# Moving the x_r product of a graph attention layer from the node phase into the rounds of edges, and loading x first

## The chip, the cores and the metric

The kernel runs on one core of a Trainium2 chip. A core has five engines with queues of their own: PE (matrix products and transposes into PSUM), DVE (vector operations), ACT (activations), POOL (general work, and here also the issuing of gathers) and SP (issuing of the other DMAs). Each engine executes its instructions in the order in which they were written down, and waits on semaphores for the others. The metric is the device time of one execution in microseconds (us). Before the change it is 4172.99 us, the median of 3 runs (4167.11 to 4175.78).

## What is computed

A graph attention layer (GATv2) with a feed-forward block, over 12500 nodes of 128 features and 400000 edges that are sorted by their destination. Cut to what matters:

```
h  = max(layernorm(x), 0)
n  = layernorm(h) * ln1_g + ln1_b
x_l = n @ W_l ;  x_r = n @ W_r          # 8 heads of 16 channels
for each edge (src -> dst), and for a loop at each node:
    m     = leaky_relu(x_l[src] + x_r[dst] + edge_attr @ W_e, 0.2)
    alpha = sum over channels of m * att, per head
a   = softmax of alpha over the edges that end in a node
h2  = h + sum of a * x_l[src] + bias
out = x + h2 + gelu(layernorm(h2) @ W1 + b1) @ W2 + b2
```

Nodes are padded to 98 tiles of 128. All of it is computed in float32; x_r is stored as three bfloat16 parts whose sum is the float32 value.

## The kernel before

The kernel has two phases. The **node phase** (lines 509 to 551) computes x_l and x_r of all nodes and writes them to DRAM: x_l to `xl_dram` (as float32, with ones behind it), x_r to `xs_dram` (as three bfloat16 parts). The **rounds of edges** (`window_edges`, lines 634 to 1132) then go over the edges, 512 in each of 782 rounds.

The order of work on every engine is written out by hand. Both phases are a loop over rounds, and a table of stages says how many rounds after its first one a group of nodes, or a batch of edges, passes through each step. Within a round the steps run in the order of the table.

In the node phase a group is four tiles (25 groups, the last with two tiles). The table `node_stages` has: `x_stats` (DVE, mean and variance of x), `x_mean`, `relu` (ACT, layer norm and relu in one operation per tile, with the row sum), `h_mean`, `h_turn` (PE, four transposes), `h_turned` (the copy out of PSUM, on DVE for odd groups and ACT for even ones), `h_square` (ACT), `h_var` (DVE), `product` (PE, against W_r and W_l side by side, 256 columns), `x_lr` (DVE, one operation per tile over 256 columns, line 477, and the store of x_l by SP, line 485) and `split` (POOL, five operations that make the three bfloat16 parts of x_r, lines 492 to 496, and their store by SP, line 497). Reciprocals and square roots (lines 545 and 547) run ahead of the stages.

Four further pieces of work are put into rounds of the node phase: `weights` (round 3), `from_first` (round 6: DVE converts the destinations, POOL takes two differences of 112x3584, line 340, and SP stores them), `fits` (round 8, DVE: does the fast path hold?) and `edge_constants` (round 10, some 20 small operations of POOL and DVE; the second of DVE, line 291, copies `we_sb`).

The loads are issued by SP in this order: x tiles 0 to 3, x tiles 4 to 15 (`load_x`), the destinations in seven DMAs (`load_dst`, of which line 240 is the large one, with 111 rows of 14 KB, lines 255 and 258 are made of single elements, and line 264 is the last), the other 82 tiles of x in six loads, then the constants (`load_consts`, with `we_sb` in line 222) and the sources of the edges. W_l, W_r, ln1_g and ln1_b are loaded by ACT's queue.

In a round of edges c, POOL gathers 4 x 128 rows of x_l by the edges' sources (`gather`, line 700, four rounds ahead of their use, into a ring of 12 buffers). SP loads, three rounds ahead, the rows of x_r that the batch can end in (`windows`; line 721 loads `xrw` from `xs_dram` at a row number held in a register). PE adds x_l, x_r and the edge term into PSUM (`combine`), ACT and DVE apply the leaky relu (`slope`, `bend`), PE, DVE and ACT compute the weights (`score`, `lowest`, `weigh`), PE transposes them (`turn`, into the ring of two banks `pt_ps`), ACT copies them out (`keep_turned`, line 795), PE sums (`collect`, round 6), DVE picks each head's own part (`own_heads`), and SP stores the result (`put`, line 826).

A second table, `steps`, finishes each group of nodes after its last edge: loop edge, softmax, feed-forward and output, in 20 rounds (`f_load` to `f_store`). Between rounds 0 and 200 the sum of all edge attributes is taken on the side.

Of the kernel before, what the change touches and what calls it, by code (L numbers as in the profile page):

```python
# [13 lines left out]
F32 = mybir.dt.float32  # L14
# [8 lines left out]
H = 8  # L23
# [96 lines left out]
def tile_gnn(  # L120
# [53 lines left out]
    flag = keep.tile([1, 1], I32, name="flag")  # L174

# [23 lines left out]
    lr_ps = pre.enter_context(tc.tile_pool(name="lr_ps", bufs=2, space=PSUM))  # L199
# [9 lines left out]
    quads = [(t, min(GN, NT - t)) for t in range(0, NT, GN)]  # L209
# [60 lines left out]
    wlr = build.tile([P, 2, C, H], F32, name="wlr")  # L270
    bw_r = build.tile([P, 2, C, H], F32, name="bw_r")

    def weights():
        mean = build.tile([P, P], F32, name="mean")
        nc.vector.memset(mean, 1.0 / P)
        b_b = build.tile([P, P], F32, name="b_b")
        nc.scalar.copy(b_b, b1n_c.to_broadcast([P, P]))
        for i, w in enumerate((wr_sb, wl_sb)):
            nc.vector.tensor_scalar(wlr[:, i], w.rearrange("p (h c) -> p c h", c=C), g1_c, None, op0=OP.mult)
        wlr_f = wlr.rearrange("p s c h -> p (s c h)")  # L280
        ps = once_ps.tile([P, 2 * P], F32, name="w_ps")
        nc.tensor.matmul(ps, mean, wlr_f, start=True, stop=True)
        nc.vector.tensor_sub(wlr_f, wlr_f, ps)
        ps = once_ps.tile([P, 2 * P], F32, name="w_ps")
        for i, w in enumerate((wr_sb, wl_sb)):
            nc.tensor.matmul(ps[:, i * P : (i + 1) * P], b_b, w, start=True, stop=True)
        nc.vector.tensor_copy(bw_r, ps.rearrange("p (s h c) -> p s c h", s=2, h=H))
# [107 lines left out]
    qs = [{"t0": t, "n": n, "h": h_sb[:, t : t + n, :]} for t, n in quads]  # L395

    roots = {}

    def col(d, name):
        d[name] = node.tile([P, GN], F32, name=f"n_{name}", bufs=5)[:, 0 : d["n"]]  # L400
        return d[name]

    def root_of(d, r, k):
        if r not in roots:
            roots[r] = (node.tile([P, 2, GN], F32, name="n_r", bufs=6), [0, 0])
        t, ns = roots[r]
        ns[k] = d["n"]
        d[f"r{k}"] = t[:, k, 0 : d["n"]]
        return d[f"r{k}"]

    def slots(r):
        if r not in roots:
            return []
        t, ns = roots[r]
        return [t] if ns == [GN, GN] else [t[:, k, 0:n] for k, n in enumerate(ns) if n]
# [14 lines left out]
    def relu(d, r):  # L430
        col(d, "sum")
        for t in range(d["n"]):
            nc.scalar.activation(
                d["h"][:, t, :], d["h"][:, t, :], AF.Relu,
                bias=d["m1"][:, t : t + 1], scale=d["r0"][:, t : t + 1], accum_out=d["sum"][:, t : t + 1],
            )

    def h_mean(d, r):
        nc.vector.tensor_scalar(d["sum"], d["sum"], -1.0 / P, None, op0=OP.mult)
# [14 lines left out]
    def h_square(d, r):  # L454
        col(d, "ssq")
        for t in range(d["n"]):
            sq = node.tile([P, P], F32, name="sq")
            nc.scalar.activation(
                sq, d["h"][:, t, :], AF.Square, bias=d["sum"][:, t : t + 1], accum_out=d["ssq"][:, t : t + 1]
            )  # L460
# [4 lines left out]
    def product(d, r):  # L465
        d["lr"] = lr_ps.tile([P, GN, 2 * P], F32, name="lr")
        for t in range(d["n"]):
            nc.tensor.matmul(
                d["lr"][:, t, :], d["hT"][:, t, :], wlr.rearrange("p s c h -> p (s c h)"), start=True, stop=True
            )  # L470

    def x_lr(d, r):
        n = d["n"]
        d["xlr"] = node.tile([P, GN, P + XW], F32, name="xlr")
        nc.gpsimd.memset(d["xlr"][:, :, 2 * P :], 1.0)
        for t in range(n):
            nc.vector.scalar_tensor_tensor(
                d["xlr"][:, t, 0 : 2 * P],
                d["lr"][:, t, :],
                d["r1"][:, t : t + 1],  # L480
                bw_r.rearrange("p s c h -> p (s c h)"),
                op0=OP.mult,
                op1=OP.add,
            )
        nc.sync.dma_start(xl_t[:, d["t0"] : d["t0"] + n, :], d["xlr"][:, 0:n, P:])

    def split(d, r):
        n = d["n"]
        xr = d["xlr"][:, 0:n, 0:P]
        parts = node.tile([P, GN, NS, P], BF16, name="parts")[:, 0:n]  # L490
        left = node.tile([P, GN, P], F32, name="left")[:, 0:n]
        nc.gpsimd.tensor_copy(parts[:, :, 0, :], xr)
        nc.gpsimd.tensor_sub(left, xr, parts[:, :, 0, :])
        nc.gpsimd.tensor_copy(parts[:, :, 1, :], left)
        nc.gpsimd.tensor_sub(left, left, parts[:, :, 1, :])
        nc.gpsimd.tensor_copy(parts[:, :, 2, :], left)
        nc.sync.dma_start(xs_t[:, d["t0"] : d["t0"] + n, :, :], parts)
# [4 lines left out]
    def clear(g):  # L502
# [12 lines left out]
        (8, x_lr),  # L515
# [5 lines left out]
        (9, split),  # L521
    )
    LAST = 9
    with tc.manual_schedule():
        make_identity(nc, ident)
        load_weights()
        load_x(0, min(GN, NT))
        load_x(GN, min(3 * GN, NT - GN))
        load_dst()
        for t in range(4 * GN, NT, 14):  # L530
            load_x(t, min(14, NT - t))
        load_consts()
        nc.gpsimd.memset(empty, 0.0)
        nc.gpsimd.memset(empty[:, :, C + 1 : SH], CAP)
        for r in range(max(len(qs), 2) + LAST + 1):
            if r == 3:
                weights()
            if r == 6:
                from_first()
            if r == 8:  # L540
                fits()
            if r == 10:
                edge_constants()
            for t in slots(r - 2):
                nc.vector.reciprocal(t, t)
            for t in slots(r - 1):
                nc.scalar.activation(t, t, AF.Sqrt)
            for late, f in node_stages:
                if 0 <= r - late < len(qs):
                    f(qs[r - late], r)  # L550
        clear(0)
# [3 lines left out]
    with tc.If(fast == 1) as cmp:  # L555
        window_edges(
            tc, n_edges, ea_t, NT, NE, NUE, ident, ident_b, wer, we_z, negrep, diag, nid, farw, bias_r, b2_r, w1_sb, w2_sb,
            cols, xl_dram, xl_t, xs_dram, xs_t, dc_dram, du_dram, state, clear, x_t, out_t, h_sb, src_sb, first_sb,
        )
    with cmp.Else():  # L560
        any_edges(
            tc, n_edges, dst, dst_tiles, ea_t, NT, NG, NCH, CPP, CP, ident, w_e, att, att_c, bias_r,
            xl_dram, xl_t, xs_t, h_sb, src_sb,
        )
        feed_forward(tc, NT, NG, ident, b2_r, w1_sb, w2_sb, cols, x_t, out_t, h_sb)
# [68 lines left out]
def window_edges(  # L634
    tc, n_edges, ea_t, NT, NE, NUE, ident, ident_b, wer, we_z, negrep, diag, nid, farw, bias_r, b2_r, w1_sb, w2_sb,
    cols, xl_dram, xl_t, xs_dram, xs_t, dc_dram, du_dram, state, clear, x_t, out_t, h_sb, src_sb, first_sb,
# [29 lines left out]
    with ExitStack() as es:  # L666
        once = es.enter_context(tc.tile_pool(name="e_once", bufs=1))
        load = es.enter_context(tc.tile_pool(name="e_load", bufs=3))
# [80 lines left out]
        def slope(c):  # L749
            d, e = pairs[c], sum(edges_of(c))  # L750
            d["zs"] = work.tile([P, EPR], F32, name="zs")
            nc.scalar.activation(d["zs"][:, :e], d["z"][:, :e], AF.Copy, scale=SLOPE)  # L752
# [292 lines left out]
        def f_store(d):  # L1045
# [10 lines left out]
            (LATE + 1, own_heads),  # L1056
            (0, combine),
# [7 lines left out]
            (5, keep_turned),  # L1065
# [42 lines left out]
        def in_round(r, table):  # L1108
            for k, f in table:
                for d in groups:  # L1110
                    if d["round"] + k == r:
                        f(d)

        CLEAR = 8
        with tc.manual_schedule():
            for r in range(-AHEAD, max(last_round, groups[-1]["round"] + 20)):
                in_round(r, early)
                for late, f in stages:
                    c = r - late
                    if 0 <= c < n_pr:  # L1120
                        f(c)
                for late, f in sum_stages:
                    i, off = divmod(r - late, SUM_STEP)
                    if off == 0 and 0 <= i < NL:
                        f(i)
                if r > 0 and r % CLEAR == 0 and r // CLEAR < NT // GT:
                    clear(r // CLEAR)
                in_round(r, steps)
                for late, f in late_stages:
                    c = r - late  # L1130
                    if 0 <= c < n_pr:
                        f(c)


def any_edges(
    tc, n_edges, dst, dst_tiles, ea_t, NT, NG, NCH, CPP, CP, ident, w_e, att, att_c, bias_r,
    xl_dram, xl_t, xs_t, h_sb, src_sb,
# [31 lines left out]
    with tc.tile_pool(name="build", bufs=1) as build:  # L1169
# [9 lines left out]
        nc.vector.scalar_tensor_tensor(pick, kh, float(LO), high, op0=OP.is_equal, op1=OP.add)  # L1179

# [302 lines left out]
```

## Time and profile before

| | value |
|---|---|
| median of 3 runs | 4172.99 us (4167.11 to 4175.78) |
| the profiled execution | 4170.51 us, of which its span 4168.6 us |
| mean granted PE clock | 0.946 |
| first 200 us: PE, DVE, ACT, POOL busy | 76.8, 135.6, 97.7, 125.9 us |
| 2000 to 2400 us: PE, DVE, ACT, POOL busy | 362.8, 236.0, 180.9, 302.6 us |
| first gather, last gather | start at 190.6 us and 4097.0 us |
| `split` on POOL, 25 of each of five operations | 28.4 + 28.4 + 15.2 + 15.2 + 15.0 us |

The span is the time from the first to the last instruction in the trace; the run's time has a little around it. A row of the profile that names a line gives the engine, the operation, what it writes and reads, how often it ran, its busy time, the mean of one in ns, and the idle time of the engine just before it with what ended that idle time ("releaser"). "issue" is waiting for which the profile shows no cause. A `q` behind an engine's name is its queue: the time in which it issues a DMA. In tables of windows, the columns are the stretch, its length, busy time of the engine with the number of its instructions, the granted PE clock, the share of the 16 DMA engines that is busy, and GB/s.

In the trace of before the row of line 721 stands 782 times, that of line 497 25 times, all of them before 190 us.

### The profile page before, as it was taken

The page shows a single profiled execution, that of the slowest core. Times are in us where ns is not written, and L with a number is a line of the kernel's source. Part 1 is how long each engine was busy: PE and PEld are TensorE (multiplying, and loading weights), DVE is VectorE, ACT ScalarE, POOL GpSimd, SP SyncE. Part 2 cuts the span into 40 slices and gives each one's busy share as a digit, 9 for nine tenths or more (in the row PEclk, how much of TensorE's full clock was granted, in tenths as well). Part 3 has the DMA queues.
Part 4 walks back from the last instruction along what each step waited for, and adds up shares of the span by engine and source line. Part 5 has one row for each costly group of instructions (what it writes and reads, how often), then busy time and mean ns, then how long its engine had stood idle before and what let it go on. Part 6 is the DMA issues. An engine that isn't in the chain of part 4 may idle for free. (4 is left out here: it accounts for less than half of the span.)

```text
span 4168.6 us, 65325 instructions
## 1 busy us (share of the span) xinstructions
PE 3562.9 (85%) x18674; PEld 2472.1 (59%) x18675; DVE 2433.0 (58%) x5279; ACT 1802.9 (43%) x3939; POOL 3073.7 (74%) x3303
## 2 busy tenths in 40 slices
PE   2488888888888898989899989889889999988985
PEld 2355555655566666666666666566666666665654
DVE  6655656656665555655555555565556564655554
ACT  4533333333334444444444444444444444434433
POOL 3977777777777777777777777777777777777772
PEclk8799999999999999999999999999999999999998
DMA  5577777666656555555655566555566565555562
GB/s 150 172 169 182 182 180 179 156 153 159 150 118 116 115 116 119 115 112 115 125 117 117 117 119 120 117 117 105 117 122 118 117 120 113 107 117 104 114 123 51
DMA packets 631298, 535.20 MB, mean 128 GB/s; under 512 B 381763, under 2 KB 520882, under 8 KB 630690
## 3 DMA queue, kind: packets, MB, share of 16 engines
q1 hardware_dynamic: 530354, 313.00, 30.8%
q0 software_dynamic: 100000, 217.80, 29.6%
q8 instruction: 153, 2.51, 0.3%
q14 instruction: 215, 1.76, 0.2%
q10 hardware_dynamic: 576, 0.13, 0.0%
HBM read 477.18 MB, written 53.34 MB: 127 GB/s over the span
## 5 line engine op out<-in xcount | busy, mean ns | idle before, releaser
L700 POOL DMA_INDIRECT xs<-xl_dram,src_sb x3125 | 2955.1, 946 | 952.5 <-issue 808.9
L782 ACT ACTIVATE p<-ab,rec 128x256 f32<-128x256 f32 x1563 | 655.2, 470 | 1678.4 <-DVE rec L771 1654.1
L813 DVE TENSOR_TENSOR own<-acc,diag 128x272 f32<-128x272 f32 x782 | 344.7, 441 | 1360.3 <-PE acc L804 1353.6
L742 PE MATMUL z<-ident,xs 128*128 128x128 f32 x3125 | 585.7, 286 | 474.2 <-DMA xs<-xl_dram,src_sb 467.6
L742 PEld LDWEIGHTS z<-ident,xs 128*128 128x128 f32 x3125 | 405.0, 142 | 945.0 <-DMA xs<-xl_dram,src_sb 563.5
L804 PE MATMUL acc<-xs,pt 128*128 128x136 f32 x6250 | 884.6, 286 | 0.2 <-DVE f_yo L1051 0.2
L746 PE MATMUL z<-ea,we_z 128*128 128x512 f32 x1564 | 859.1, 633 | 0.0
L804 PEld LDWEIGHTS acc<-xs,pt 128*128 128x128 f32 x6250 | 812.5, 197 | 0.4 <-PE pt_ps L790 0.4
L764 PE MATMUL ab<-m,negrep 128*128 128x512 f32 x1564 | 801.1, 594 | 0.0
L752 ACT ACTIVATE zs<-z 128x512 f32<-128x512 f32 x782 | 474.7, 607 | 494.7 <-PE z L746 453.8
L790 PEld LDWEIGHTS pt_ps<-ident,p 128*128 128x128 f32 x3125 | 417.9, 149 | 453.6 <-issue 424.2
L771 DVE TENSOR_REDUCE rec<-ab 128x2 f32<-128x512 f32 x781 | 540.6, 692 | 135.9 <-PE ab L764 128.5
L757 DVE TENSOR_TENSOR m<-z,zs 128x512 f32<-128x512 f32 x782 | 532.2, 681 | 54.2 <-ACT zs L752 54.1
L790 PE MATMUL pt_ps<-ident,p 128*128 128x128 f32 x3125 | 498.2, 285 | 1.7 <-ACT pt L795 1.7
L795 ACT COPY pt<-pt_ps 128x512 f32<-128x512 f32 x782 | 457.6, 585 | 0.0
L819 DVE TENSOR_REDUCE rec<-own 128x34 f32<-128x272 f32 x782 | 341.0, 436 | 26.6
L746 PEld LDWEIGHTS z<-ea,we_z 128*128 128x128 f32 x1564 | 314.6, 201 | 35.7
L764 PEld LDWEIGHTS ab<-m,negrep 128*128 128x128 f32 x1564 | 301.8, 193 | 37.4 <-issue 0.7
L745 PE MATMUL z<-ne,xrw 128*128 128x512 bf16 x782 | 311.3, 398 | 0.0
L728 DVE TENSOR_SCALAR ne<-dlw,nid 112x512 bf16<-112x512 bf16 x782 | 288.5, 369 | 25.6 <-DMA dlw<-du_dram 25.6
L763 PE MATMUL ab<-ne,farw 128*128 128x512 bf16 x782 | 300.9, 385 | 0.0
L839 DVE TENSOR_REDUCE part<-ea_s 128x1 f32<-128x1024 f32 x98 | 118.5, 1209 | 0.0
(165 smaller groups left out, 1619.0 us busy)
## 6 DMA issues: line engine op xcount, KB each, us to landing
dlw<-dc_dram SPq DMA_DIRECT2D x196, 384.0 KB
ea<-in_ea_t SPq DMA_DIRECT2D x196, 256.0 KB
ea_s<-in_ea_t SPq DMA_DIRECT2D x98, 512.0 KB
xs<-xl_dram,src_sb POOLq DMA_INDIRECT x3125
state<-rec SPq DMA_DIRECT2D x1563, 9.0 KB
xrw<-xs_dram SPq DMA_DIRECT2D x782, 24.0 KB
state<-empty SPq DMA_DIRECT2D x28, 504.0 KB
st<-state SPq DMA_DIRECT2D x48, 288.0 KB
```

What stands on the lines that cost most here:

```text
L700: nc.gpsimd.indirect_dma_start(out=xs[:, j, :], out_offset=None, in_=xl_dram, in_offset=bass.IndirectOffsetOnAxis(ap=src_sb[:, c * KP + j ...
L742: nc.tensor.matmul(z[:, j * P : (j + 1) * P], d["xs"][:, j, 0:P], ident, start=(j == 0), stop=False, is_transpose=True)
L746: nc.tensor.matmul(z[:, :e], we_z[:, c % QP, :], d["ea"][:, :e], start=False, stop=True)
L752: nc.scalar.activation(d["zs"][:, :e], d["z"][:, :e], AF.Copy, scale=SLOPE)
L757: nc.vector.tensor_tensor(d["m"][:, :e], d["z"][:, :e], d["zs"][:, :e], op=OP.max)
L764: nc.tensor.matmul(ab[:, :e], negrep.rearrange("p n h -> p (n h)"), d["m"][:, :e], start=False, stop=True)
L771: nc.vector.tensor_reduce(d["rec"][:, :, CX], d["ab"].rearrange("p (u e) -> p u e", e=U), AX.X, OP.min)
L782: nc.scalar.activation(d["p"][:, us], d["ab"][:, us], AF.Exp, bias=d["rec"][:, i, CX:SH], scale=-1.0)
L790: nc.tensor.transpose(d["pt_ps"][:, js], d["p"][:, js], ident)
L795: nc.scalar.copy(d["pt"][:, :e], d["pt_ps"][:, :e])
L804: nc.tensor.matmul(d["acc"][:, i, :], d["pt"][:, j * P : (j + 1) * P], d["xs"][:, j, :], start=(j == js[0]), stop=(j == js[-1]),)
L813: nc.vector.tensor_tensor(own[:, :nu], d["acc"][:, :nu].rearrange("p u (c h) -> p u c h", h=H), diag[:, None].to_broadcast([P, nu, CX, H]) ...
```

## The change

The node phase keeps the x_l half of the product, 128 columns. Its stage `split` is gone; `x_lr` becomes `x_l`. It now keeps two things per group that lived in rotating buffers before: the reciprocal roots (`roots_sb`) and the negative mean of h (`mean_sb`).

A new function `xr_steps` computes x_r of a group from them in eight steps: `norm` (one small DVE product, four ACT operations), `turn` (PE, four transposes), `turned` (ACT, the copy with the affine part of the norm), `times` (PE, four products with W_r), `first` (ACT copy and DVE subtraction), `second` (ACT copy), `third` (DVE subtraction) and `store` (SP). Group 0 goes through them in rounds 8 to 15 of the node phase. The others go through them in the rounds of edges, one step a round, in the ring `pt_ps`: group k starts in round 32k - 18, so that its store is issued two rounds ahead of the first window that can need it.

The load of dst is put behind all loads of x. `edge_constants` moves from round 10 to round 7, `from_first` from 6 to 10, `fits` from 8 to 12. In the rounds of edges `keep_turned` is put ahead of `combine`. The pool `load` shrinks from three buffers to two, `zs` from three to two, and `lr_ps` grows from two to three banks of half the size in use.

```diff
-    lr_ps = pre.enter_context(tc.tile_pool(name="lr_ps", bufs=2, space=PSUM))
+    lr_ps = pre.enter_context(tc.tile_pool(name="lr_ps", bufs=3, space=PSUM))
...
     def product(d, r):
-        d["lr"] = lr_ps.tile([P, GN, 2 * P], F32, name="lr")
+        d["lr"] = lr_ps.tile([P, GN, P], F32, name="lr")
...
-                d["xlr"][:, t, 0 : 2 * P],
+                d["xl"][:, t, 0:P],
...
-    def split(d, r):
-        n = d["n"]
-        xr = d["xlr"][:, 0:n, 0:P]
-        parts = node.tile([P, GN, NS, P], BF16, name="parts")[:, 0:n]
-        left = node.tile([P, GN, P], F32, name="left")[:, 0:n]
-        nc.gpsimd.tensor_copy(parts[:, :, 0, :], xr)
-        nc.gpsimd.tensor_sub(left, xr, parts[:, :, 0, :])
-        nc.gpsimd.tensor_copy(parts[:, :, 1, :], left)
-        nc.gpsimd.tensor_sub(left, left, parts[:, :, 1, :])
-        nc.gpsimd.tensor_copy(parts[:, :, 2, :], left)
-        nc.sync.dma_start(xs_t[:, d["t0"] : d["t0"] + n, :, :], parts)
+    def xr_steps(pool, bank):
+        def norm(d):
+            off = pool.tile([P, GN], F32, name="xr_off")[:, 0 : d["n"]]
+            nc.vector.tensor_mul(off, d["mean"], d["r1"])
+            hn = tile_of(d, "hn", 0)
+            for t in range(d["n"]):
+                nc.scalar.activation(
+                    hn[:, t, :], d["h"][:, t, :], AF.Identity, bias=off[:, t : t + 1], scale=d["r1"][:, t : t + 1]
+                )
+        def turn(d):
+            d["b"] = bank()
+            for t in range(d["n"]):
+                nc.tensor.transpose(d["b"][:, t * P : (t + 1) * P], d["hn"][:, t, :], ident)
+        def turned(d):
+            nc.scalar.activation(
+                tile_of(d, "hT", 1).rearrange("p t f -> p (t f)"),
+                d["b"][:, 0 : d["n"] * P], AF.Identity, bias=b1n_c, scale=g1_c,
+            )
+        def times(d):
+            d["b"] = bank()
+            for t in range(d["n"]):
+                nc.tensor.matmul(
+                    d["b"][:, t * P : (t + 1) * P], d["hT"][:, t, :], wr_c.rearrange("p c h -> p (c h)"),
+                    start=True, stop=True,
+                )
+        def first(d):
+            n = d["n"]
+            xr = d["b"][:, 0 : n * P].rearrange("p (t f) -> p t f", f=P)
+            d["parts"] = pool.tile([P, GN, NS, P], BF16, name="xr_parts")[:, 0:n]
+            nc.scalar.copy(d["parts"][:, :, 0, :], xr)
+            nc.vector.tensor_sub(tile_of(d, "left", 0), xr, d["parts"][:, :, 0, :])
+        def second(d):
+            nc.scalar.copy(d["parts"][:, :, 1, :], d["left"][:, 0 : d["n"]])
+        def third(d):
+            nc.vector.tensor_sub(d["parts"][:, :, 2, :], d["left"][:, 0 : d["n"]], d["parts"][:, :, 1, :])
+        def store(d):
+            nc.sync.dma_start(xs_t[:, d["ts"], :, :], d["parts"])
+        return norm, turn, turned, times, first, second, third, store
...
-        load_dst()
         for t in range(4 * GN, NT, 14):
             load_x(t, min(14, NT - t))
+        load_dst()
         load_consts()
...
-            if r == 6:
+            if r == 7:
+                edge_constants()
+            if r == 10:
                 from_first()
-            if r == 8:
+            if r == 12:
                 fits()
-            if r == 10:
-                edge_constants()
...
+            if 0 <= r - LAST < len(first_xr):
+                first_xr[r - LAST](qs[0])
...
-        load = es.enter_context(tc.tile_pool(name="e_load", bufs=3))
+        load = es.enter_context(tc.tile_pool(name="e_load", bufs=2))
...
-            d["zs"] = work.tile([P, EPR], F32, name="zs")
+            d["zs"] = work.tile([P, EPR], F32, name="zs", bufs=2)
...
             (LATE + 1, own_heads),
+            (5, keep_turned),
             (0, combine),
...
-            (5, keep_turned),
             (-1, place),
...
+        xr_steps = xr_steps(fin, lambda: ps2.tile([P, EPR], F32, name="pt_ps"))
+        per_node = edges_per_node(NT, n_edges)
+        for d in qs[1:]:
+            first = (d["t0"] * P - CW) * per_node // U - SPARE
+            d["round"] = first // UP - WAHEAD - len(xr_steps) - 1
+            assert d["round"] >= -AHEAD
...
                 in_round(r, steps)
+                in_round(r, enumerate(xr_steps), qs[1:])
```

## The prediction

> **What bounds the kernel now.** I read the page's busy times first, then the gathers by stretch, then who waited for whom, then the timeline before the first gather. PE is the busiest engine on the page, and yet the waits show that it is POOL's gathers that pace everything.
>
> ```profile
> PE 3562.9 (85%) x18674; PEld 2472.1 (59%) x18675; DVE 2433.0 (58%) x5279; ACT 1802.9 (43%) x3939; POOL 3073.7 (74%) x3303
> L700 POOL DMA_INDIRECT xs<-xl_dram,src_sb x3125 | 2955.1, 946 | 952.5 <-issue 808.9
> ```
>
> In the windows of line 700 (busy time, instructions, granted clock, DMA share, GB/s) the gathers keep one pace, with or without sums of edge attributes (up to 1200 us) and finishing steps beside them:
>
> ```profile
> 600.00:1000.00 400.00, 302.43 (x321) 0.96 0.71 163
> 1400.00:1800.00 400.00, 302.45 (x321) 0.95 0.60 120
> 3000.00:3400.00 400.00, 302.57 (x320) 0.96 0.60 118
> ```
>
> In the waits, no pause before a gather is longer than 0.3 us, and PE stops for gathered rows:
>
> ```profile
> POOL xs L700 <- issue: 808.9, 2654, 0.3
> PE z L742 <- DMA xs<-xl_dram,src_sb: 467.6, 343, 27.9
> ```
>
> The first gather starts at 190.6 us and the last at 4097.0: 3906.4 us for 3124 steps, 1.2505 us each. So span = start of the first gather + 3906.4 + tail (4168.6 - 4097.0 = 71.6). Only the start can give much, and its timeline (start, duration) shows POOL splitting x_r right up to it:
>
> ```profile
> 177.51 0.61 POOL L492 CAST parts<-xlr 128x512 bf16<-128x512 f32 x1
> 181.93 0.61 POOL L492 CAST parts<-xlr 128x512 bf16<-128x512 f32 x1
> 188.71 0.40 POOL L496 CAST parts<-left 128x256 bf16<-128x256 f32 x1
> 189.45 0.93 POOL L683 MEMSET xrw<- 128x128 bf16 x6 [0.34 <-issue]
> 190.56 1.12 POOL L700 DMA_INDIRECT xs<-xl_dram,src_sb  x1 [0.17 <-issue]
> ```
>
> One group of four tiles costs POOL 4.42 us (177.51 to 181.93); ACT had finished at 161, DVE's last x_lr at 176. The early timeline shows two more stops, the load of dst and a pair of POOL subtractions:
>
> ```profile
> 7.64 22.74 SPq L258 DMA_DIRECT2D lu<-in_dst  x1
> 31.90 12.58 SPq L232 DMA_DIRECT2D h_sb<-in_x  x6
> 36.98 0.29 DVE L421 BATCH_NORM_STATS2 s<-h_sb 128x6 f32<-128x128 f32 x1 [18.94 <-DMA h_sb<-in_x]
> 43.32 12.28 POOL L340 TENSOR_TENSOR dlb<-df 112x3584 bf16<-112x3584 f32 x2 [41.36 <-DVE n_r L545]
> 43.35 6.15 DVE L426 SCALAR_TENSOR_TENSOR n_m<-n_stats,n_r 128x4 f32<-128x4 f32 x1
> 49.13 0.59 SPq L222 DMA_DIRECT2D we_sb<-in_w_e  x1
> ```
>
> **Removed from the node phase.** POOL's split (28.4 + 28.4 + 15.2 + 15.2 + 15.0 = 102 us) goes; next late are ACT and DVE. ACT per group: relu 4 x 0.478, squares 4 x 0.388, half a copy of 0.47, a root 0.1: 3.8 us. DVE per group: statistics 1.79 (67.29 to 69.08), small operations 0.44, half a copy 0.3, and x_l. Four x_lr operations took 1.57 start to start, 0.394 each. 128x512 against 128x256 additions (0.700 and 0.433) make 128 elements worth 0.133, so the narrower x_l is 0.26 each (bounds 0.20, a 128x128 row, and 0.39), 1.04 in all: 3.57 us. DVE's small operations, raised by POOL to 0.50 us in the mean (L426), fall back to 0.16. PE's product halves and was not the bound.
>
> **x first, dst behind it, constants behind dst.** x's first 1.05 MB arrived by 6 us; its other 5.37 MB ran at 347 GB/s, so all x is in by 6 + 15.5 = 21.5 us and the 18.94 us wait goes. The dst loads then start: in the trace they took from 6.5 to 30.4 us, 24 us, at 79 to 86 GB/s and a DMA share of 0.18 to 0.20. Now 21.5 + 24 = 45.4. All this while SP is stopped in line 258's issue, and queued behind that are the constants: 1.5 us for line 264 and its wait, four columns 1.9, att 0.7, we_sb 0.6, landing 2: **we_sb is there at 52 us**. But edge_constants is now at round 7, which DVE reaches at about 24 us (rounds 0 to 3 end at 15 as before, then 3 us each), and its second operation copies we_sb. DVE stops there for some 28 us, ACT and PE behind it: the stop is moved, not removed. The cost from both sides: dst overlapping x wholly would land we_sb near 33, other queue delays at 65. A rule here: the Trainium skill, "DMA: Bandwidth & Descriptors", section on the anatomy of one DMA, fits a transfer as 2 us plus bytes over 436 GB/s (fitted on POOL's queue). For dst's 1.55 MB it gives 5.6 us, not 24, and a first gather 18 us earlier. The row decides, since it is this very transfer: I take 52.
>
> **The node phase after.** we_sb 52; rest of edge_constants 8.1 us in the trace (75.84 to 83.97), of which some 2.3 came from POOL's split beside it (128x128 at 1.18 where its like takes 0.22), so 5.9: round 7 begins at 57.9. Round 7 without x_l 2.5, rounds 8 and 9 3.6 each plus 0.2: 67.7. Round 10: df 2.2, DVE held by the two subtractions 12.3 (as at 43.35), 3.6: 85.7. Round 11: 89.3. Round 12: fits 6.7 + 3.6: 99.6. Rounds 13 to 24 at ACT's 3.8: 145. Group 0's x_r adds 1.6 us of DVE and 3.8 of ACT in rounds 8 to 15, mostly under those stops: +1, 146. Then the pipe drains: relu and squares of the last groups 3.8 + 3.8 + 2.9 + 1.9 + 1.2 = 13.6, three x_l stages with the root between them 3.4: 163. Last x_l store issued and landed 2.5 (estimated from the first x load, issued 0.77, used at 3.92): **first gather at 166**, 24.6 us earlier. POOL's xrw memsets are done by then.
>
> **Added to the rounds**, 24 groups, one each 32 rounds (160 us). ACT: four normalisations 1.9 (L986 0.50), 0.8 (L1001), two copies 0.6 each (L795): 3.9 us, on an engine 45% busy. DVE: 0.2 + 2 x 0.7 (L1049). PE: four transposes and four 128x128 products, 0.6 each (L790's four 0.60): 1.2 us, against 428 us of waiting for gathers between 230 and 4090, 17 us in each 160. The bank comes from the pt_ps ring of two; line 795's copy is put ahead of the round's PE work so that the next transpose finds one free. There are 12 row buffers; a buffer is free 6 rounds after its turn on PE, and POOL issues some 1.3 rounds before rows are there, so PE can fall back by 12 - 6 - 1.3 = 4.7 rounds (23 us) before a gather waits: bumps of 1 to 2 us never reach POOL. Without that cover all 24 x 1.2 = 29 us would show. The smaller rings (load 2, zs 2) cost nothing: a window of edges is loaded at round c-3, when its buffer was last read at c-5.
>
> SP: each store of parts (0.37 us to issue) waits for third on DVE, for earlier xrw reads, and the next xrw load waits for the store, 384 KB: some 5 us landing, 5 to 15 us of stop, bounds 1 and 20. Behind it queue puts and xrw loads. SP already stops 313.6 us at 24 stores of f_yo, 13 on average and 31.5 at most, without a gather waiting. So nothing, with that as the near row.
>
> A rule that speaks against the change: the Trainium skill, "SBUF — State Buffer", section "two separate sides", says that DVE operations with two SBUF inputs or in a two-port mode lock GpSimd out of the port [...]. third has two SBUF inputs: by the rule up to 24 x 0.7 = 17 us on the gathers, and a time of 4163. The lock is real in this trace (L426 at 6.15 us beside L340). But 3125 gathers have a median of 944 ns and a minimum of 940, beside 782 each of L728 and L819 on SBUF. I take 0.
>
> **Sum.** 166 + 3906.4 + 71.6 = 4144 span; the profiled run had 1.9 us around its span, 4146. That run was 2.5 us under the median of 4172.99, which less 24.6 is 4148.4. I forecast **4147 us**, 0.6% faster.
>
> **Rivals.** (1) The constants come later still, or DVE, ACT and PE lose more by the stop at round 7: first gather at 185 to 195, time 4165 to 4175, the same. For it: SP's queue is fully serial. Against: it needs we_sb 20 us later than the rows give. (2) Slower: the xs stores in the rounds. If a store's waits hold SP so long that xrw comes late by more than the 23 us in which PE and POOL can drift, POOL stops. From 1.0 us per group (24.6 / 24) it cancels the gain; at 3 us it gives 4146 + 72 = 4218. For it: the load of xs_dram is by a register, so it must wait for any store. Against: f_yo's 31.5 us stop. (3) The port lock: 4163. (4) Constants early, as by the DMA rule: first gather near 148, 4128.
>
> **How the numbers follow.** Main case 0.70, within 4135 to 4160. (4) 0.08, (3) 0.04, (1) 0.08, (2) 0.10. A measurement here tells 0.2% (8 us) from no change. Faster: main, (4), (3) and a little of (1): 0.83; same: 0.07; slower: 0.10. The range reaches to (4) and (3): 4128 to 4166.
>
> **What would show it.** First gather at 166 (155 to 178); 320 or 321 gathers in each 400 us; DVE idle some 28 us before L291's successor, released by the load of we_sb; no POOL work between the two subtractions and the xrw memsets but iotas and small memsets; POOL's pauses still at 0.3 us; ACT, not POOL, busy to the end of the node phase. I am wrong if gathers pause near the xs stores, if their pace is off 1.25 us, or if the first one starts after 182.

## The result and the profile after

| | before | after |
|---|---|---|
| median, beside each other on one chip (5 runs each) | 4173.31 us (4167.11 to 4175.78) | 4152.08 us (4150.08 to 4155.11) |
| ratio, 95% interval | | 0.995 (0.9936 to 0.9965) |
| profiled execution: start of the first gather | 190.6 us | 164.1 us |
| first to last gather | 3906.4 us | 3917.7 us |
| tail behind the last gather's start | 71.6 us | 67.5 us |
| span (their sum) | 4168.6 us | 4149.3 us |

The change makes the kernel 21.2 us faster; 24.6 were forecast from the profiled execution, 26 from the median. The gain is the earlier start (-26.5 us); the gathers gave 11.3 us of it back and the tail came out 4.1 us shorter: -19.3 us of span. The experiments ran on three chips, and on the first two every kernel, the one before too, takes some 700 to 760 us longer (between gathers POOL stops there 390 to 399 times for over 1 us, on the other chips never), so each time below stands only beside the kernel before on its own chip.

On the page of after, POOL has lost its split, ACT and PE have the work of x_r, and the gathers still carry the row with the most idle time behind "issue":

```profile
PE 3587.8 (86%) x18966; PEld 2503.7 (60%) x18967; DVE 2445.8 (59%) x5354; ACT 1927.1 (46%) x4112; POOL 2985.3 (72%) x3178
...
L747 POOL DMA_INDIRECT xs<-xl_dram,src_sb x3125 | 2966.3, 949 | 954.3 <-issue 820.1
```

ACT's busy time grew by 124 us (1802.9 to 1927.1) and PE's by 25, and no pause of POOL came of it. The mean gather is 949 ns, where it was 946. Over 3125 gathers these 3 ns are some 9 to 11 us: a number that looks like rounding takes back four tenths of what the earlier start gains. The windows of the gathers by stretch (busy time, instructions, granted clock, DMA share, GB/s) show that it is spread over the whole run:

```profile
600.00:1000.00 400.00, 302.56 (x320) 0.96 0.73 166
1400.00:1800.00 400.00, 302.76 (x320) 0.96 0.61 123
3000.00:3400.00 400.00, 303.05 (x319) 0.97 0.60 121
```

There are 320, 320 and 319 gathers where 321, 321 and 320 stood before, at a clock that differs by 0.01 at most. The waits of after (total, times, longest) tell which waits are not the cause:

```profile
POOL xs L747 <- issue: 820.1, 2690, 0.3
...
PE z L789 <- DMA xs<-xl_dram,src_sb: 410.0, 368, 4.4
...
DVE wer L294 <- DMA we_sb<-in_w_e: 27.7, 1, 27.7
...
SPq L1099 <- DVE f_yo L1098: 283.3, 23, 30.5
SPq L540 <- DVE xr_parts L537: 112.9, 20, 8.1
```

POOL pauses for 0.3 us between gathers and never longer, as before. SP does stop at the new stores of x_r (line 540), up to 8.1 us, but no gather waits longer for it. PE still waits 410 us for gathered rows, 58 less than before, so the work added there has eaten from the cover and not gone through it. And DVE stops once for 27.7 us at the copy of `we_sb`. The timeline of after (start, duration) shows that stop, and what leads to it:

```profile
17.86 1.87 SPq L244 DMA_DIRECT2D dc<-in_dst  x1
...
22.10 23.88 SPq L262 DMA_DIRECT2D lu<-in_dst  x1
...
50.20 0.59 SPq L226 DMA_DIRECT2D we_sb<-in_w_e  x1
...
52.48 0.27 DVE L294 COPY wer<-we_sb 128x128 f32<-128x128 f32 x1 [27.71 <-DMA we_sb<-in_w_e]
...
57.73 0.17 DVE L590 RECIPROCAL roots_sb<-roots_sb 128x4 f32<-128x4 f32 x1
...
160.46 0.61 DVE L478 SCALAR_TENSOR_TENSOR xl<-lr,roots_sb,bl_r 128x128 f32<-128x128 f32 x2 [0.20 <-DVE roots_sb L590]
161.21 0.94 POOL L730 MEMSET xrw<- 128x128 bf16 x6 [1.13 <-DVE xl L478]
...
164.08 1.10 POOL L747 DMA_INDIRECT xs<-xl_dram,src_sb  x1 [1.93 <-DMA xl_dram<-xl]
```

SP is held from 22.10 to 45.98 us in one issue behind the large load of dst, and `we_sb`, a load of 0.59 us, is queued behind it. (From 24 to 42 us the share of busy DMA engines is 0.19, about 3 of 16; a load of dst that keeps more of them busy was not tried.) The chain to the first gather is now x_l, its store and 1.93 us of landing; the split is nowhere in it.

### The profile page after: what moved, and what is told of

It reads as the page before. It is cut to its first block, busy times and chain, and to the rows that moved or that the text cites. A ratio compares the mean times of both kernels' runs of the same rounds, so it can differ in the third digit from the quotient of the medians.

```text
span 4149.3 us, 63978 instructions
## 1 busy us (share of the span) xinstructions
PE 3587.8 (86%) x18966; PEld 2503.7 (60%) x18967; DVE 2445.8 (59%) x5354; ACT 1927.1 (46%) x4112; POOL 2985.3 (72%) x3178
## 4 chain that ended last, share of the span: by engine, by line
PE 32%; POOL 26%; DMA 24%; issue 14%; DVE 0%; ACT 0%; POOLq 0%; SPq 0%; DVEq 0%; ACTq 0%
POOL xs L747 26%; DMA xs<-xl_dram,src_sb 23%; PE z L793 7%; PE acc L851 7%; PE ab L811 5%; PE z L789 4%; PE pt_ps L837 4%; PE z L792 2%; PE ab L810 1%; PE acc L1084 1%; PE acc L1059 0%; PE acc L954 0%; PE acc L937 0%; DMA state<-rec 0%; PE pt_ps L521 0%
## 5 line engine op out<-in xcount | busy, mean ns | idle before, releaser
L793 PE MATMUL z<-ea,we_z 128*128 128x512 f32 x1564 | 849.4, 626 | 0.0
L799 ACT ACTIVATE zs<-z 128x512 f32<-128x512 f32 x782 | 471.9, 603 | 25.6 <-PE z L793 25.6
```

Of the source, the lines that this page charges most:

```text
L793: nc.tensor.matmul(z[:, :e], we_z[:, c % QP, :], d["ea"][:, :e], start=False, stop=True)
```

## The experiments

Five questions were open. Is it x_r's move alone that gains, or also the new order of loads (runs 1, 2, 6)? What is the stop for `we_sb` worth (3, 10)? Where do the gathers lose 11 us, by the port that `third` takes (4, 7), or by something that comes and goes between executions (5, 11)? Do the mended versions add up (8, 9)? "Excess" below is what gathers of over 0.95 us take beyond 0.95, summed: 5.6 us before, 12.7 after.

| run | first gather | first to last | its time | before beside it | ratio (95%) |
|---|---|---|---|---|---|
| e1, old order | 156.6 | 4592.8 | 4835.83 | 4873.18 | 0.9924 (0.991 to 0.9937) |
| e2, x behind dst | 162.9 | 4598.2 | 4843.34 | 4873.18 | 0.9938 (0.9924 to 0.9952) |
| e3, two loads ahead | 141.8 | 4592.4 | 4821.67 | 4873.18 | 0.9895 (0.988 to 0.9911) |
| e4, third from PSUM | 166.4 | 4594.0 | 4845.94 | 4873.18 | 0.9948 (0.9934 to 0.9961) |
| e5, after | 163.3 | 4648.0 | 4895.57 | 4931.19 | 0.993 (0.9916 to 0.9943) |
| e6, order alone | 199.2 | 4655.5 | 4939.65 | 4931.19 | 1.0017 (1.0007 to 1.0026) |
| e7, third twice | 164.4 | 4648.6 | 4899.62 | 4931.19 | 0.9936 (0.9923 to 0.995) |
| e8, e3 and e4 | 145.2 | 4644.7 | 4874.72 | 4931.19 | 0.9886 (0.9871 to 0.9901) |
| e9, best | 143.2 | 3909.4 | 4123.81 | 4172.42 | 0.9882 (0.9867 to 0.9897) |
| e10, as e3 | 142.0 | 3915.0 | 4127.74 | 4172.42 | 0.9891 (0.9875 to 0.9906) |
| e11, after | 163.6 | 3914.8 | 4149.43 | 4172.42 | 0.9944 (0.9931 to 0.9958) |

**e1: only x_r's move.** The loads and the early pieces of work return to their old order.

```diff
+        load_dst()
         for t in range(4 * GN, NT, 14):
             load_x(t, min(14, NT - t))
-        load_dst()
         load_consts()
...
-            if r == 7:
-                edge_constants()
-            if r == 10:
+            if r == 6:
                 from_first()
-            if r == 12:
+            if r == 8:
                 fits()
+            if r == 10:
+                edge_constants()
```

> Only the move of x_r is kept: dst is loaded ahead of the late tiles of x again, and from_first, fits, edge_constants are back in rounds 6, 8, 10. Theory (the first gather's start decides, and the order of loads is worth nothing or less, since it only turns the wait for x into DVE's 27.7 us stop for we_sb): DVE waits for x until 37 us, is held by the two subtractions until 55.5, then has no stop; first gather at about 155 us, 9 earlier than in the changed kernel, time 4143. Rival (loading x first is a part of the gain, worth the 18.9 us wait that it removes): first gather at about 183, time 4171.

The first gather starts at 156.6 us, as the theory had it and not at the rival's 183: some 7 us earlier than with the new order (163.3 to 164.1 in the three traces of after). In the waits of DVE in e1, up to its first gather, the stop for x is back, and none for `we_sb` is there:

```profile
DVE s L423 <- DMA h_sb<-in_x: 26.0, 3, 20.3
```

So x_r's move alone takes the start from 190.6 to 156.6 us, 34.0 us, and the rest of the change gives back 7.5 of them. The kernel before was traced on the first chip alone; on this chip its time stands 37.4 us above e1's, which agrees.

**e2: only the loads put back.** The load of dst goes ahead of the late tiles of x again; the rounds stay as changed.

```diff
+        load_dst()
         for t in range(4 * GN, NT, 14):
             load_x(t, min(14, NT - t))
-        load_dst()
```

> The changed kernel with dst loaded ahead of the late tiles of x again, rounds as changed. Theory: DVE reaches round 7 at 44 us instead of 24.6 and stops there until we_sb lands at about 52, as before; first gather at 164, time 4152, no difference beyond 3 us. Rival (x first is worth its 18.9 us): first gather at 183, time 4171.

162.9 us, again with the theory. The waits of DVE in e2 up to the first gather show why "x first" buys nothing:

```profile
DVE s L423 <- DMA h_sb<-in_x: 25.6, 3, 19.9
DVE wer L294 <- DMA we_sb<-in_w_e: 6.2, 1, 6.2
```

Two stops of 19.9 and 6.2 us stand where after has one of 27.7. The loads have one queue, and DVE needs both x and `we_sb`; putting x ahead only changes which of them it waits for. Of the 7.5 us that after gives back, 6.3 lie between e1 and e2, which differ in the rounds alone: `edge_constants` in round 7 waits for `we_sb`, and in round 10 it does not. The order of the loads costs the rest, 0.4 to 1.2 us by the three traces of after.

**e3 and e10: `att` and `we_sb` ahead of dst.** Here the small loads no longer queue behind the large one:

```diff
     def load_consts():
-        nc.sync.dma_start(att_c, ...)
-        nc.sync.dma_start(we_sb, ...)
...
+    def load_first():
+        nc.sync.dma_start(att_c, ...)
+        nc.sync.dma_start(we_sb, ...)
...
+        load_first()
         load_dst()
         load_consts()
```

> The changed kernel with the loads of att and we_sb ahead of the load of dst. Theory: we_sb is there at about 24 us, DVE's stop of 27.7 us goes and becomes one of some 4 us for dst in round 10; first gather at about 142, time 4130. Rival (ACT and dst set the pace of the node phase, the stop is hidden): first gather at 160 to 164, time 4148 to 4152.

> The changed kernel with only the loads of att and we_sb moved ahead of dst, beside the one above. First gather at 141.8 us as in its first trace; 22 us less than the changed kernel.

141.8 and 142.0 us, 22 us earlier than after, and beside after on one chip 21.7 us less time (e10 against e11). The timeline of DVE in e3 shows what is late next:

```profile
44.75 2.16 DVE L341 CAST df<-dc 112x3841 f32<-112x3841 int32 x1 [4.94 <-DMA dc<-in_dst]
...
47.06 6.12 DVE L430 SCALAR_TENSOR_TENSOR n_m<-n_stats,roots_sb 128x4 f32<-128x4 f32 x1
...
53.17 6.13 DVE L466 TENSOR_SCALAR roots_sb<-n_ssq 128x4 f32<-128x4 f32 x1
```

The stop of 27.7 us has become one of 4.94, for dst itself; and two small operations that take 0.16 us elsewhere take 6.12 and 6.13, which is the time of POOL's two differences beside them.

**e4: the last remainder read from PSUM.** All of the splitting happens in one round, with the remainder kept in the PSUM bank, so that no subtraction has two operands in SBUF (the memory of all tiles that are not in PSUM).

```diff
             nc.scalar.copy(d["parts"][:, :, 0, :], xr)
-            nc.vector.tensor_sub(tile_of(d, "left", 0), xr, d["parts"][:, :, 0, :])
+            nc.vector.tensor_sub(xr, xr, d["parts"][:, :, 0, :])
+            nc.scalar.copy(d["parts"][:, :, 1, :], xr)
+            nc.vector.tensor_sub(d["parts"][:, :, 2, :], xr, d["parts"][:, :, 1, :])
...
         def second(d):
-            nc.scalar.copy(d["parts"][:, :, 1, :], d["left"][:, 0 : d["n"]])
+            pass
         def third(d):
-            nc.vector.tensor_sub(d["parts"][:, :, 2, :], d["left"][:, 0 : d["n"]], d["parts"][:, :, 1, :])
+            pass
```

> The changed kernel with the remainders of x_r kept in the PSUM bank, so that no subtraction of the split has two operands in SBUF; the three steps of the split stand in one round. Theory (the subtraction third, with both operands in SBUF, holds up POOL's gather beside it): no gather above 1.25 us, the gathers' sum 7 us less, time 4145. Rival (the longer gathers come from the traffic of the xs stores and xrw loads): gathers of 1.3 to 1.7 us remain, time 4152.

The rows of the gathers (minimum, median and maximum in ns, first and last start), in e1 and in e4:

```profile
L747 POOL DMA_INDIRECT xs<-xl_dram,src_sb x3125: 938/944/1556, 156.6 to 4749.4; - x196
```

```profile
L749 POOL DMA_INDIRECT xs<-xl_dram,src_sb x3125: 939/947/1277, 166.4 to 4760.4; - x196
```

The longest gather falls from 1556 to 1277 ns (1250 were expected), and the excess to 2.0 us, against 5.2 to 6.3 in e1 to e3: most of the lengthening is `third`'s. The expected 7 us of time could not be made out on that chip, where first to last differs by 5.8 us between e2 and e3, which share the rounds. And the edit has a price in group 0, in the node phase: there DVE is late, and ACT has to wait for it, as the waits of ACT in e4 show:

```profile
ACT xr_parts L532 <- DVE w_ps L531: 8.0, 1, 8.0
```

**e5 and e11: after again,** to have it beside the other kernels of each chip.

> The changed kernel, unchanged, so that the others of this call and the four before can be set beside it. First gather at 164 us as in its first trace. Theory: the gain over the kernel before is the earlier start, 26.5 us, less the longer gathers where nothing else stops POOL. If the chip is the one on which before takes 4873 us, POOL stops there some 400 times for 2 us anyway: time 4844 to 4847; if it is like the first, 4152.

> The changed kernel on the same chip as the two above. First gather at 163 to 164 us; before less 20 to 30 us.

The first gather stands at 163.3 and 163.6 us, so that much is the kernel's. The tail is 68.9 in e11, 69.6 in e9 and 70.8 in e10, so much of the -4.1 us of the first table can be scatter between executions (before was traced once). The median gather is 944, 945 or 947 ns, whatever the kernel: 944 in e1, e2, e3, e7 and e8, 947 in e4, e5 and e6, 945 in after, e9, e10 and e11. One ns is 3 us.

The loss in the gathers is not seen on every chip. On e5's, first to last is 4655.5 us in e6, which leaves x_r in the node phase, and 4644.7 to 4648.6 in e5, e7 and e8, which don't; e5 is 35.6 us faster than before there, for a start that is some 27 us earlier. `third` lengthens gathers there too (17 of them, 5.1 us in e5), so something else outweighs it on that chip; what it is stays open.

**e6: the order without x_r's move.** The kernel before, with the load of dst behind x and the three pieces of work in rounds 7, 10 and 12.

```diff
-        load_dst()
         for t in range(4 * GN, NT, 14):
             load_x(t, min(14, NT - t))
+        load_dst()
...
-            if r == 6:
+            if r == 7:
+                edge_constants()
+            if r == 10:
                 from_first()
-            if r == 8:
+            if r == 12:
                 fits()
-            if r == 10:
-                edge_constants()
```

> The kernel before, with only the order of loads and the rounds of from_first, fits and edge_constants of the change; x_r stays in the node phase. Theory (POOL's split, 4.42 us a group, decides when the gathers start): first gather at 186 to 190 us, time 0 to 4 us under before. Rival (the order is a part of the gain): first gather at 172 or less, 19 us under before.

Missed: 199.2 us, and 8.5 us slower than before. The timeline of POOL in e6 shows that the split does decide, as expected, but later:

```profile
64.30 0.61 POOL L492 CAST parts<-xlr 128x512 bf16<-128x512 f32 x1 [60.65 <-DVE xlr L477]
...
70.84 12.28 POOL L340 TENSOR_TENSOR dlb<-df 112x3584 bf16<-112x3584 f32 x2 [2.10 <-DVE df L336]
83.12 0.61 POOL L492 CAST parts<-xlr 128x512 bf16<-128x512 f32 x1
...
194.98 0.40 POOL L492 CAST parts<-xlr 128x256 bf16<-128x256 f32 x1
```

After the first group POOL turns to its two differences, and only at 83.12 to the other 24 groups. From there to 194.98 stand 23 whole groups, 101.7 us at 4.42, and 10 us that the expectation had left out. They are `fits` on DVE: POOL's cast beside it takes 4.15 us instead of 0.61, and then POOL waits 5.82 us for the x_lr behind it, as the timeline of DVE and POOL in e6 shows:

```profile
91.02 4.06 DVE L351 CUSTOM_DVE_ANT_0 junk<-df 112x3584 f32<-112x3584 f32 x1
91.40 4.15 POOL L496 CAST parts<-left 128x512 bf16<-128x512 f32 x1
...
106.04 0.61 POOL L492 CAST parts<-xlr 128x512 bf16<-128x512 f32 x1 [5.82 <-DVE xlr L477]
```

So the order costs 8.6 us where POOL splits (190.6 to 199.2) and 7.5 us where it does not (e1 against 164.1): it is no help in either kernel.

**e7: `third` twice.** After, with the subtraction issued a second time.

```diff
         def third(d):
             nc.vector.tensor_sub(d["parts"][:, :, 2, :], d["left"][:, 0 : d["n"]], d["parts"][:, :, 1, :])
+            nc.vector.tensor_sub(d["parts"][:, :, 2, :], d["left"][:, 0 : d["n"]], d["parts"][:, :, 1, :])
```

> The changed kernel with the subtraction third done twice in place. Theory (it holds up the gather beside it, 17 of 24 times in the trace): the gathers' excess over 0.95 us grows by another 7 us, time +7 where POOL never stops otherwise, and less where it does. Rival (the xs traffic lengthens gathers): no change beyond 2 us.

Missed: the excess is 6.7 us, against 6.5 in e5, and first to last 4648.6 against 4648.0. The time is 4.0 us longer than e5's all the same, which fits neither side; in the traces 1.1 of it is a later start and 0.9 a longer tail. The timeline of DVE and POOL in e7 tells why the excess does not grow:

```profile
505.50 0.68 DVE L537 TENSOR_TENSOR xr_parts<-xr,xr_parts 128x512 bf16<-128x512 f32 x1
505.89 1.10 POOL L748 DMA_INDIRECT xs<-xl_dram,src_sb  x1 [0.30 <-issue]
506.21 0.69 DVE L538 TENSOR_TENSOR xr_parts<-xr,xr_parts 128x512 bf16<-128x512 f32 x1
507.29 0.95 POOL L748 DMA_INDIRECT xs<-xl_dram,src_sb  x1 [0.30 <-issue]
```

The gather of 505.89 is lengthened by the first subtraction; then it runs, all through the second one, and the next gather starts at 507.29, when the second has ended (506.90). A doubled hold costs only where a gather begins inside the second subtraction. The experiment had been meant to double a cost per instruction, and the cost is not per instruction.

That can be read from after itself. The timeline of DVE and POOL in after, around four of the 24 subtractions:

```profile
1718.71 1.69 POOL L747 DMA_INDIRECT xs<-xl_dram,src_sb  x1 [0.30 <-issue]
1718.89 0.68 DVE L537 TENSOR_TENSOR xr_parts<-xr,xr_parts 128x512 bf16<-128x512 f32 x1
...
1881.41 0.94 POOL L747 DMA_INDIRECT xs<-xl_dram,src_sb  x1 [0.30 <-issue]
1881.59 0.68 DVE L537 TENSOR_TENSOR xr_parts<-xr,xr_parts 128x512 bf16<-128x512 f32 x1
...
2200.55 0.69 DVE L537 TENSOR_TENSOR xr_parts<-xr,xr_parts 128x512 bf16<-128x512 f32 x1
2200.62 1.44 POOL L747 DMA_INDIRECT xs<-xl_dram,src_sb  x1 [0.30 <-issue]
...
3323.33 1.52 POOL L747 DMA_INDIRECT xs<-xl_dram,src_sb  x1 [0.30 <-issue]
3323.35 0.69 DVE L537 TENSOR_TENSOR xr_parts<-xr,xr_parts 128x512 bf16<-128x512 f32 x1
```

Start plus duration gives the gathers' ends: 1720.40, 2202.06, 3324.85. The subtractions end at 1719.57, 2201.24, 3324.04: 0.83, 0.82 and 0.81 us earlier. For 16 of the 24 the lengthened gather ends 0.81 to 0.83 us behind the subtraction, wherever it began; `third` itself takes no longer for it. Together these 16 take 22.08 us, which is 7.0 more than 16 gathers of 0.945. The gather of 1881.41 had begun 0.18 us ahead of its subtraction and got through. The one of 1718.71 had the same lead and did not; at its start DVE ran the `ne` comparison of line 775 (once a round; here 1718.64 to 1718.98), which most likely held it. The other traces that issue `third` once agree: every gather that it holds and that had begun ahead of it has `ne` at its start, and without `ne` even one that began 0.004 us ahead got through in 0.947 us (in e11, at 2035.27; the subtraction took 0.72 us there). `ne` holds gathers by itself too: in the kernel before, 73 of the 79 gathers over 0.96 us lie beside that comparison, where one in four would by its number (782 among 3125).

Whether it is the second operand in SBUF can also be read from after, in the subtraction of `first`. It has the same size and length, but one operand in PSUM:

```profile
906.07 0.68 DVE L531 TENSOR_TENSOR xr<-pt_ps,xr_parts 128x512 f32<-128x512 f32 x1
906.16 0.94 POOL L747 DMA_INDIRECT xs<-xl_dram,src_sb  x1 [0.31 <-issue]
```

Ten gathers begin in the first 0.5 us of a `first`, and all take 0.94 to 0.95 us; twelve begin in the first 0.5 us of a `third`, and all take 1.10 to 1.48. In e9 both subtractions read PSUM, and one of them writes bfloat16 as `third` does: 35 gathers begin so, 15 of them in that one, and none takes over 0.95.

**e8: e3 and e4 together,** with `from_first` in round 11 and `fits` in round 13 besides.

```diff
+        load_first()
         load_dst()
...
-            if r == 10:
+            if r == 11:
                 from_first()
-            if r == 12:
+            if r == 13:
                 fits()
```

> The changed kernel with att and we_sb loaded ahead of dst, the remainders of x_r kept in PSUM, and from_first and fits one round later (11 and 13), when dst is there. Theory: first gather at about 140 us, 24 earlier than the changed kernel, no gather above 1.3 us: time 24 us less than the changed kernel where POOL stops anyway, 31 less where it doesn't. Rival (ACT at 3.8 us a group sets the end): 142 or later.

Missed by 5 us: 145.2, which falls under the rival's "142 or later". The waits of DVE in e8 up to the first gather name a wait that neither part had:

```profile
DVE xl L480 <- DMA xl_dram<-xl: 5.3, 1, 5.3
```

A buffer of x_l is written again only when its last store has landed. The gathers did what was expected: none over 1.102 us, excess 1.2.

**e9: the best version.** e3; the remainders in PSUM, but in the rounds of edges alone (group 0 keeps the old way, hence no wait for DVE there); and the two differences of destinations on DVE.

```diff
+        load_first()
         load_dst()
...
-            nc.gpsimd.tensor_tensor(
+            nc.vector.tensor_tensor(
...
-    def xr_steps(pool, bank):
+    def xr_steps(pool, bank, in_bank=True):
...
-            nc.vector.tensor_sub(tile_of(d, "left", 0), xr, d["parts"][:, :, 0, :])
+            if in_bank:
+                nc.vector.tensor_sub(xr, xr, d["parts"][:, :, 0, :])
+                nc.scalar.copy(d["parts"][:, :, 1, :], xr)
+                nc.vector.tensor_sub(d["parts"][:, :, 2, :], xr, d["parts"][:, :, 1, :])
+            else:
+                nc.vector.tensor_sub(tile_of(d, "left", 0), xr, d["parts"][:, :, 0, :])
...
-    first_xr = xr_steps(node, lambda: once_ps.tile([P, GN * P], F32, name="w_ps"))
+    first_xr = xr_steps(node, lambda: once_ps.tile([P, GN * P], F32, name="w_ps"), False)
```

> The changed kernel with att and we_sb loaded ahead of dst, the two differences of from_first on DVE instead of POOL (some 3.9 us each, the 3584-element operation of fits, in place of 12.3 us in which POOL's hold DVE), and the remainders of x_r in PSUM in the rounds of edges only. Theory: first gather 141.8 - 4.5 = 137 us, no gather above 1.3 us, time 5 to 8 us under the kernel with only the constants moved. Rival (ACT's 3.8 us a group sets the end): first gather 141 to 142, time 1 to 3 us under it.

4123.81 us: 48.6 under before, 25.6 under after and 3.9 under e10, all on one chip. The start missed its 137 (143.2). The timeline of DVE in e9, then its waits up to the first gather:

```profile
47.63 7.69 DVE L345 TENSOR_TENSOR dlb<-df 112x3584 bf16<-112x3584 f32 x2
```

```profile
DVE df L341 <- DMA dc<-in_dst: 5.7, 1, 5.7
...
DVE xl L480 <- DMA xl_dram<-xl: 5.0, 1, 5.0
```

DVE does the differences in 7.69 us, where POOL had held it for 12.3, but the time that it wins is given back at the same store of x_l as in e8. Past that stop it is the rival's engine that sets the pace: from 80 to 120 us ACT is busy for 39.96 of the 40. The gain over e10 is the gathers': 3909.4 against 3915.0, excess 3.8 against 9.6, none over 1.145 us where e10 has 1.623. In e10 `third` holds ten gathers, 3.8 us; that the rest of the difference is the edit's too is not shown.

## Why the prediction was right, and what was off in it

- **The bound** held: on the first chip POOL issues gathers back to back from the first one on, and the time is start, gathers and tail. PE, ACT, SP and DVE took in the new work (ACT's instructions alone add up to 95 us more) without a pause of POOL over 0.3 us.
- **The start** came out step by step: "we_sb is there at 52 us" (its first reader runs at 52.48); a DVE stop of some 28 us (27.7); round 7 at 57.9 (57.73); x_l at 0.26 us a tile (four in 1.12 us, 0.28); ACT, not POOL, busy to the end of the node phase (45.96 of the 46 us from 100 to 146); last x_l at 163 (161.1); first gather at 166 (164.1). Of the two prices for the load of dst, the row's 24 us was right: SP came free at 45.98 us, where 45.4 was forecast, and the fit of the Trainium skill's page "DMA: Bandwidth & Descriptors", section on the anatomy of one DMA, made for POOL's queue, which gave an estimate of 5.6 us, would have had `we_sb` there 18 us sooner.
- **The slower rival**, SP held by the stores of x_r, fell. They do stop SP, up to 8.1 us, within the "5 to 15 us" of the estimate, and no gather waits longer for it.
- **The constants early** was a rival of 4128 us that needed a faster load of dst. It did not happen by itself; e10 makes it happen by the order of the queue, and lands on 4127.74. That the numbers meet so closely is partly luck: e10 starts at 142.0 us where the rival had 148, and its gathers take 8.6 us more than the 3906.4 that the rival kept.
- **The term that was mis-sized** is "I take 0" for the port that `third` shares with POOL. It is 7.0 us: 0 by the row, up to 17 by the rule of the Trainium skill's page "SBUF — State Buffer", section "two separate sides". There the lock goes to whichever operation starts first, for its whole length, and a DVE operation with two SBUF inputs takes it only against a GpSimd operation that reads SBUF. The prediction left that condition out; a gather, which reads its row numbers from `src_sb`, meets it. The rule's mechanism holds here: `first`, with one operand in PSUM, holds no gather, and e4 and e9, which take the second SBUF operand away from `third`, take the long gathers beside it away (that what is locked is a port is the page's account; the runs show only which operations hold which). The prediction's size, every subtraction's whole length, does not hold: a gather that is under way isn't stopped, and one that begins inside loses what is left of the operation less some 0.12 us (it ends 0.82 us behind it, and takes 0.945 when nothing holds it), on average 0.44 us for 16 of 24. The row was misread. Median and minimum of 3125 gathers cannot show a hold that reaches a few per cent of them; their maximum (1223 ns) and the 79 over 0.96 us, most of them beside the `ne` comparison, were in the trace of before and did. Two of the forecast's own signs show the miss: 319 gathers in the last of the three stretches where 320 or 321 were named, and a pace of 1.254 us where 1.2505 stood.
- **What stays open.** Of the 11.3 us in the gathers 7 are `third`'s. The other 4 fit 1 ns in the median gather, which stands between 944 and 947 ns in these traces, and in the three of after at 945, 947 and 945; the tail too moves, by up to 3 us on the chips without stops. Neither was explained. The excess itself varies, 12.7 in after and 9.4 in e11, of which 7.0 and 5.3 are `third`'s: the two don't fall on the gathers at the same moments.

The forecast of 4147 is 5 us under the 4152.08 measured. In the spans, 4144 against 4149.3, the start is 1.9 us earlier than forecast, the gathers are 11.3 us longer and the tail 4.1 shorter: the forecast's number is as close as it is because two smaller errors hide half of the large one. "x loaded first", which the forecast passed as a stop that is "moved, not removed", deserved a comparison with not moving it: the new order costs 7.5 us, 6.3 of them by the rounds and the rest by the loads.

## What to carry to other kernels

When one engine paces the whole run at a constant rate, the time is where that rate starts, plus whatever lengthens single steps: look at the maximum and the count of the slow ones, since the median hides them. Before moving a large load, list what stands behind it on its queue and which engine needs the smallest of these first; here two small loads put ahead of one of 24 us gained 21.7 us, about as much as the whole change. And where an edit removes a wait, ask for the second wait behind it: `we_sb` behind x, dst behind `we_sb`, and the store of x_l behind dst came up one after the other.

## What the runs showed of the hardware

A gather that starts while a DVE subtraction with two SBUF operands runs is held: in after it ends 0.81 to 0.83 us behind the subtraction, in 12 of the 12 cases that begin in its first 0.4 us, and in 4 that begin up to 0.19 us ahead of it beside `ne`. Two that begin 0.63 and 0.65 us into it are not lengthened, and neither is one that begins 0.18 us ahead of it without `ne`. With one operand in PSUM the same subtraction holds no gather (10 of 10 in after, 35 of 35 in e9). A second subtraction issued right behind, 0.03 us later, does not hold the gather again. `ne`, which has one tensor operand, holds gathers as well: in before, the 30 that begin 0.10 to 0.15 us behind its start take 1.04 us in the mean and 1.22 at most.

Between elementwise operations the cost is larger, in both directions: beside a POOL subtraction of 6.1 us, DVE operations of 0.16 us take 6.12 and 6.13 (in e3), and beside a DVE operation of 4.06 us (`fits`, in e6) a POOL cast of 0.61 us takes 4.15.
